# A graph attention layer on one core: query products in a bank of their own, their parts spread over two steps

## The chip, the cores and the metric

The kernel runs on one core of one Trainium2 chip. The metric is the device time of one execution in microseconds. Three runs of the kernel before gave a median of 1546.13 us (1540.45 to 1554.27).

## The reference

A graph has 3125 nodes with 128 features `x` and 100000 edges, sorted by their destination `dst`; each edge has a source `src` and one of five relations. Per relation there are query, key and value weights for eight heads of 16. The layer is an attention of every node over its incoming edges, separately for each relation, then a projection, a residual and two layer norms:

```
for r in range(5):
    q, k, v = x[dst] @ W_Q[r], x[src] @ W_K[r], x[src] @ W_V[r]
    logits  = (q * k).sum(-1) / 4 + attn_bias[r]          # masked to edges of relation r
    e       = exp(logits - segment_max(logits, dst))
    out    += segment_sum(e / (segment_sum(e, dst) + 1e-12) * v, dst)
h = out.reshape(3125, 128) @ out_proj_w.T + out_proj_b + x
y = layernorm(h) * ln_gamma + ln_beta
result = layernorm(x + y)
```

## The kernel before

All that counts is in `windowed_path`. It has a preamble, a main loop of 66 steps, and an end.

**Preamble.** Weights and `x` are loaded and turned on PE. `table(b)` makes, for each of 25 blocks of 128 nodes, a row of key and value for every node and relation, and SP stores it to the DRAM table `kv_d`. Small side jobs hang between the blocks by the dictionary `side`, among them `query_weights` (the turned query weights, L324 on PE and L328 on ACT) and `project_weights`. Behind the table the queries of the first four blocks are made: product on PE, then the three bf16 parts into which a float32 query is split (first: cast of the product; second: cast of the remainder; third: remainder minus second part), stored to `q_d`.

**Main loop.** Edges come in tiles of 128, four tiles to a group, three groups (twelve tiles) to a step; the last two steps have two groups. Several steps are under way at once; step `k` of the Python loop issues, for its own and its neighbours' groups:

- `products(k)` (DVE, L799), `logits(k)` (L832), `closed_lanes(k)` (L809): query times key, reduced to logits, lanes of other relations closed; `turn_logits` (PE, L860) and `keep_logits` (ACT, L875) turn them so that edges lie along the free axis; `scans(k)` (DVE, L881 and L884) and `less_max` (L891) give each segment's maximum and subtract it; `exps` (ACT, L899) and `turn_exps` (PE, L906) make the exponentials and turn them back.
- `weights(k-1)` (ACT, L916) and `weigh(k-1)` (DVE, L922) copy the exponentials and multiply the gathered values by them, into `wv`. `places` (ACT, L931 and L934) makes selection matrices, and `sums` (PE, L952 and L947) adds each group's rows up by segment, into the PSUM tile `both`.
- `norm(k-2)` (DVE, L964, L966, L968) divides by the totals, `relations(k-2)` (PE, L981) adds the five relations, `by_node(k-2)` (ACT, L985) copies the result to its nodes.
- `gather(k+3)` (POOL, L707): twelve indirect DMAs, one for each tile, that read rows of `kv_d`. The ring has a slot less than would be needed to be free of the current step: the last of the twelve writes to a slot that `weigh(k-1)` reads, and waits for it.
- `spot` (DVE, L764) and `spread_q` (PE, L778) spread the query rows over the edges of a tile. `take(k)` has SP load what they need, three steps ahead: the keys `kt` (L635), twelve pieces of query rows `qw` out of `q_d` (L642), the masks `mk` (L756). SP works through its queue in order.

The queries of blocks 4 to 24 are made inside the loop. `q_at` names the step at which `turn_q` and `turned` transpose the block (L717, L722). `half(k)` says that the next step handles its first three relations and the step after that the other two. In a step with a half, `remainder` and `second_part` stand between `logits` and `closed_lanes`, and `third_part` between `norm` and `relations`; the product and the first cast were issued at the end of the step before:

```
        if after[0] is not None:
            queries(*after)          # PE  L728, PSUM tile prq
            first_part(*after[:2])   # ACT L733
```

`remainder` is L737 (DVE), `second_part` L742 (ACT), `third_part` L746 (DVE). After the second half, `store_q` (SP, L608) writes the block's query rows to `q_d`. Blocks whose sums are complete are finished in the loop too: `project` (PE, L992), `residual`, `roots` (ACT, L1022), `norms`, `store_z` (SP, L1058). The order inside a step is written out by hand; each engine works through its instructions in that order, held by semaphores only.

PSUM has eight banks: three for the spread queries `qe`, two for `lt`, one for `ex`, one for `both`, and one, tagged `fin`, which transposes, query products, relation sums and projections take in turn.

**End.** After the loop the last two blocks' sums, norms and stores follow one another.

Of the kernel before, what the change touches and what calls it, by code (L numbers as in the profile page):

```python
# [17 lines left out]
P = 128  # L18
# [3 lines left out]
R = 5  # L22
# [112 lines left out]
def windowed_path(  # L135
# [111 lines left out]
    src_r = load_rows("src_r", src, 0)  # L247
    typ_r = load_rows("typ_r", edge_type, 0)
    load_x(10, 17)
    nc.sync.dma_start(wnq, w_q.rearrange("r k h d -> (r k) (h d)"))  # L250
# [151 lines left out]
    def table(b, xT):  # L402
        n_ = P if b < NT - 1 else 64
        kvs = work.tile([P, R * 2, H], F32, name="kvs", bufs=3)
        wf = wkv.rearrange("h r s c -> h (r s) c")
        for n, (c0, c1) in enumerate(((0, 4), (4, 8), (8, 10))):
# [8 lines left out]
        nc.sync.dma_start(  # L415
            kv_d[b * P * R : (b * P + n_) * R, :].rearrange("(p r) c -> p (r c)", r=R),
            kvs[:n_].rearrange("p s h -> p (s h)"),
        )

    kvrow = load.tile([HG, 2, GE], F32, name="kvrow")  # L420
    keyr = load.tile([HG, 2, GE], F32, name="keyr")
# [90 lines left out]
    def count_short():  # L512
        nc.vector.tensor_reduce(vio[:HG, 1:2], srt[:, :, : GE - SEG], AX.XY, ALU.add)
# [50 lines left out]
    def types(s, rs):  # L564
# [7 lines left out]
    side = {  # L572
        1: [begins],
        2: [weights_a],
        3: [lambda: query_weights(0)],
        4: [lambda: query_weights(8), weights_b],
        5: [lanes],
        6: [keys_a],
        7: [keys_c],
# [8 lines left out]
        16: [types(0, (0,)), project_weights],  # L588
        17: [types(0, (1,))],
        18: [types(0, (2,))],  # L590
        19: [types(0, (3,))],
# [88 lines left out]
    checks()  # L680
    pre.close()
# [31 lines left out]


    def turn_q(b):
        tp = ps.tile([P, P], F32, name="tp", tag="fin")
        nc.tensor.transpose(tp, xn[:, b, :], ident)  # L717
        live["tp", b] = tp

# [3 lines left out]

    def queries(b, c0, c1):
        if c0 == 0:
            live["q3", b] = flow.tile([P, R, 3, H], BF16, name="q3", bufs=1)
        pr = ps.tile([P, c1 - c0, H], F32, name="prq", tag="fin")
        nc.tensor.matmul(pr, live["xT", b], wq[:, c0:c1, :], start=True, stop=True)  # L728
        live["pr", b, c0] = pr, live["q3", b][:, c0:c1], c1 - c0
# [171 lines left out]
    def turn_exps(k):  # L901
        n = len(groups(k))
        ls = live.pop(("ls", k))
        ex = ps.tile([P, T * G3, HEADS], F32, name="ex")[:, : T * n]
        for t in range(T):
            nc.tensor.matmul(  # L906
                ex.rearrange("p (i t) k -> p t i k", t=T)[:, t],
                ls[: n * LANES, t * P : (t + 1) * P],
                gather_heads[: n * LANES, :n], start=True, stop=True,
            )  # L910
        live["ex", k] = ex
# [24 lines left out]

    def sums(g):
        k, i = AT[g]
        if i == 0 and ("both", k) not in live:
            live["both", k] = ps.tile([P, G3 * (PW + HEADS)], F32, name="both")  # L940
        pp = total(k)[:, i]
        at, wv = live.pop(("at", g)), live["wv", k]
        end = tiles_of(g) - 1
        for t in range(end + 1):
            if g and t == end:
                last, j = AT[g - 1]
                nc.tensor.matmul(  # L947
                    pp[:R], over[:, g, :],
                    live["wv", last][:, T * j + T - 1, :],
                    start=False, stop=False,  # L950
                )
            nc.tensor.matmul(  # L952
                pp[:WR], at[:, t, :], wv[:, T * i + t, :], start=(t == 0), stop=(t == end)
            )
        if i == 0:
            live.pop(("wv", k - 1), None)

    def total(k):
        return live["both", k][:, : G3 * PW].rearrange("p (g c) -> p g c", g=G3)

    def norm(k):
        n, pp = len(groups(k)), total(k)
        tot = live["both", k][:, G3 * PW :].rearrange("p (g c) -> p g c", g=G3)[:WR, :n]
        nc.vector.tensor_scalar_add(tot, pp[:WR, :n, H:PW], 1e-12)  # L964
        den = flow.tile([WR, G3, HEADS], F32, name="den", bufs=1)[:, :n]
        nc.vector.reciprocal(den, tot)  # L966
# [7 lines left out]
        live["o5", k] = o5  # L974
        live.pop(("both", k))

    def relations(k):
        o5 = live.pop(("o5", k))
        live["nodes", k] = nodes = ps.tile([P, G3, WN], F32, name="nodes", tag="fin")
        for i, g in enumerate(groups(k)):  # L980
            nc.tensor.matmul(nodes[:, i], o5[:, i], rsum[:WR], start=True, stop=True)  # L981

# [72 lines left out]

    def store_z(b):
        n = min(P, N - b * P)
        nc.sync.dma_start(out[b * P : b * P + n, :], live.pop(("z", b))[:n, :])  # L1058
# [5 lines left out]
    block_at = {k: b for b, k in done_at.items() if k < NST}  # L1064
    rest = [b for b in range(NT) if done_at[b] >= NST]


    q_from = {}
# [31 lines left out]

    for k in range(NST):
        new, old = k >= 1, k >= 2
        q0, (q, c0, c1), after = q_at.get(k), half(k), half(k + 1)
        done, rooted = block_at.get(k), block_at.get(k - 1)
        place_g, sum_g = list(groups(k - 1)), list(groups(k - 1))

# [46 lines left out]
        sum_next()  # L1153
# [19 lines left out]
    begun = rest[0] - 1  # L1173
    assert rest == [NT - 2, NT - 1] and done_at[begun] < k
    assert full_at(rest[0]) < G0[k] and len(groups(k)) == 2
    room = ps.tile([P, T * G3, H], F32, name="qe").rearrange("p n h -> p (n h)")
    live["both", k] = room[:, : G3 * (PW + HEADS)]
    places(G0[k])
    weights(k)
    places(G0[k] + 1)  # L1180
    norm(k - 1)
    relations(k - 1)
    by_node(k - 1)
    weigh(k)
    project(rest[0])
    for b in rest:
        shifted(b)
    roots(rest[0], 1, 2)
    norms(rest[0])
    store_z(begun)  # L1190
    sums(G0[k])
    residual(rest[0])
    roots(rest[0], 0, 1)
    sums(G0[k] + 1)
    norms(rest[0])
    norm(k)
    relations(k)
    by_node(k)
    project(rest[1])
    residual(rest[1])  # L1200
    roots(rest[1])
    norms(rest[1])
    store_z(rest[0])
    roots(NT, 1, 2)
    norms(NT)
    store_z(rest[1])

    ctx.close()

# [504 lines left out]
```

## Time and profile before

| what | value |
|---|---|
| median of three runs | 1546.13 us (1540.45 to 1554.27) |
| the profiled execution | 1546.65 us, its span 1544.9 us |
| preamble, to the first scan | 0 to 178.0 us |
| main loop, first to last scan | 178.0 to 1518.7 us |
| end | 1518.7 to 1544.9 us |
| busy: PE, DVE, POOL, ACT | 878.7, 883.9, 757.4, 620.8 us |
| mean granted TensorE clock | 0.667 |

PE, DVE, ACT, POOL and SP are the engines; PEld is PE's loading of weights. A row of a group names line, engine, operation, the tiles written and read, their shape and the count; then the busy time and the mean ns of one; then how long the engine had been idle just before such instructions and what ended that. A row of a timeline has the start, the duration, the engine, the line and the tiles, and in brackets the idle time before it and its releaser. "SPq" is SP's DMA queue. A row of windows gives a stretch, its length, and each engine's busy time. "remote" means that no event in the profile explains the release.

### The profile page before, as it was taken

How to read it: one execution, taken by the hardware profiler on the slowest of the kernel's cores; microseconds unless marked ns; L12 is line 12 of the kernel's file. 1: busy time of each engine (PE TensorE's matmuls, PEld its weight loads, DVE VectorE, ACT ScalarE, POOL GpSimd, SP SyncE). 2: the span in 40 equal slices, each digit the busy share in tenths (PEclk: the TensorE clock that was granted, in tenths of full speed). 3: DMA queues.
4: the chain of work that ended last, by engine and by line, in shares of the span. 5: the costliest groups of instructions: out<-in, count | busy, mean ns of one | idle time of the engine just before them, and what ended most of it. 6: DMA issues, size and time to landing. Idle time of an engine off the chain costs nothing. (4 is left out here: it accounts for less than half of the span.)

```text
span 1544.9 us, 17015 instructions
## 1 busy us (share of the span) xinstructions
PE 878.7 (57%) x4515; PEld 659.4 (43%) x4515; DVE 883.9 (57%) x1259; ACT 620.8 (40%) x1699; POOL 757.4 (49%) x850
## 2 busy tenths in 40 slices
PE   7920346545665555655556555565556655566686
PEld 4510234433444444443444434454444443344464
DVE  4831345645666545665556646565555655565686
ACT  3420233433453434443443434443433443444464
POOL 2067145445555555545555545555455545555510
PEclk9965566666666666666666666666666666666677
DMA  8663355434444445544454445544455434454420
GB/s 229 280 185 112 76 124 148 126 109 126 129 130 120 121 123 133 133 116 121 131 138 118 117 122 128 139 123 119 117 135 129 131 108 121 132 130 125 120 55 8
DMA packets 177099, 196.48 MB, mean 127 GB/s; under 512 B 122143, under 2 KB 137130, under 8 KB 176874
## 3 DMA queue, kind: packets, MB, share of 16 engines
q0 software_dynamic: 37728, 102.55, 25.4%
q1 hardware_dynamic: 138718, 91.65, 20.9%
q10 hardware_dynamic: 548, 1.11, 0.2%
q8 instruction: 38, 0.62, 0.2%
q14 instruction: 67, 0.55, 0.1%
HBM read 164.80 MB, written 30.40 MB: 126 GB/s over the span
## 5 line engine op out<-in xcount | busy, mean ns | idle before, releaser
L707 POOL DMA_INDIRECT kv_early<-kv_d,idx x474 | 453.2, 956 | 470.4 <-DVE wv L922 266.0
L952 PE MATMUL both<-wv,at 128*125 128x136 f32 x1552 | 393.5, 409 | 57.7 <-DVE wv L922 45.1
L707 POOL DMA_INDIRECT kv_late<-kv_d,idx x308 | 294.1, 955 | 250.1 <-DVE wv L922 163.3
L952 PEld LDWEIGHTS both<-wv,at 128*125 128x125 f32 x1552 | 316.7, 284 | 140.7 <-issue 75.3
L860 PE MATMUL lt<-ident,lx 128*120 128x128 f32 (+2 forms) x396 | 80.7, 361 | 374.9 <-DVE both L964 263.5
L931 ACT ACTIVATE at<-row_at,nkey 128x125 f32<-128x125 f32 x782 | 246.9, 388 | 0.0
L860 PEld LDWEIGHTS lt<-ident,lx 128*120 128x120 f32 (+2 forms) x396 | 51.5, 177 | 404.3 <-issue 357.9
L737 DVE TENSOR_TENSOR prq<-prq,q 128x384 f32<-128x384 f32 (+1 forms) x42 | 21.0, 500 | 349.6 <-ACT q L733 286.3
L733 ACT CAST q<-prq 128x384 bf16<-128x384 f32 (+1 forms) x42 | 17.9, 426 | 457.1 <-remote 416.4
L981 PE MATMUL nodes<-rsum,o 125*128 125x25 f32 x392 | 92.5, 380 | 119.1 <-DVE o L968 51.0
L981 PEld LDWEIGHTS nodes<-rsum,o 125*128 125x128 f32 x392 | 84.6, 312 | 132.0 <-DVE o L968 55.0
L934 ACT ACTIVATE at<-at 128x500 f32<-128x500 f32 x196 | 121.4, 619 | 6.2
L881 DVE TENSOR_TENSOR_SCAN lt<-mk,lt 120x640 f32<-120x640 bf16 (+1 forms) x66 | 98.3, 1489 | 36.2 <-DMA mk<-msk_d 35.7
L832 DVE TENSOR_REDUCE lt<-prod 128x96 f32<-128x1536 f32 (+1 forms) x66 | 115.0, 1742 | 2.2
L778 PE MATMUL qe<-qw,hot 120*128 120x128 bf16 x784 | 60.8, 221 | 74.6 <-DMA qw<-q_d 47.4
L947 PE MATMUL both<-wv,over 128*5 128x136 f32 x386 | 102.4, 360 | 0.0
L884 DVE TENSOR_TENSOR_SCAN lt<-mk,lt 120x640 f32<-120x640 bf16 (+1 forms) x66 | 98.7, 1495 | 2.2
L799 DVE TENSOR_TENSOR prod<-kv_early,qe 128x1536 f32<-128x1536 f32 (+3 forms) x53 | 71.3, 1346 | 41.6 <-DMA kv_late<-kv_d,idx 38.6
L916 ACT COPY wv<-ex 128x96 f32<-128x96 f32 (+1 forms) x66 | 15.1, 229 | 178.6 <-remote 165.2
L778 PEld LDWEIGHTS <-hot 120*128 120x128 bf16 x784 | 51.2, 105 | 77.3 <-issue 77.0
L922 DVE TENSOR_TENSOR wv<-kv_early,ex 128x1536 f32<-128x1536 f32 (+1 forms) x40 | 69.3, 1733 | 25.2 <-ACT wv L916 25.2
L875 ACT COPY ls<-lt 120x512 f32<-120x512 f32 (+1 forms) x66 | 39.0, 591 | 103.0 <-PE lt L860 99.1
(169 smaller groups left out, 1087.2 us busy)
## 6 DMA issues: line engine op xcount, KB each, us to landing
qw<-q_d SPq DMA_DIRECT2D x784, 30.0 KB
kt<-key_d SPq DMA_DIRECT2D x63, 360.0 KB
kv_d<-kvs SPq DMA_DIRECT2D x24, 640.0 KB
q_d<-q SPq DMA_DIRECT2D x25, 480.0 KB
mk<-msk_d SPq DMA_DIRECT2D x64, 150.2 KB
kv_early<-kv_d,idx POOLq DMA_INDIRECT x474
kv_late<-kv_d,idx POOLq DMA_INDIRECT x308
out<-z SPq DMA_DIRECT2D x24, 64.0 KB
```

The costliest lines, as they stand in the source:

```text
L707: nc.gpsimd.indirect_dma_start(out=kv[:, at, :], out_offset=None, in_=kv_d[:, :], in_offset=bass.IndirectOffsetOnAxis(ap=idx[:, q % T, q / ...
L778: nc.tensor.matmul(dest[j], hot[:, j * P : (j + 1) * P], qw[:, j, :], start=True, stop=True)
L799: nc.vector.tensor_tensor(prod[:, n:m], kv[:, c0:c1, :H], qe[:, n:m], op=ALU.mult)
L832: nc.vector.tensor_reduce(lg, heads(live.pop(("prod", k))[:, :m]), AX.X, ALU.add)
L860: nc.tensor.transpose(live["lt", k][: n * LANES, c : c + w], live["lx", k][p : p + w, j : j + n].rearrange("p g r k -> p (g r k)"), ident[ ...
L881: nc.vector.tensor_tensor_scan(lt, mk[:n, :WIDE], lt, -BIG, op0=ALU.add, op1=ALU.max)
L884: nc.vector.tensor_tensor_scan(lt[:, ::-1], mk[:n, WIDE:0:-1], lt[:, ::-1], -BIG, op0=ALU.add, op1=ALU.max)
L931: nc.scalar.activation(at[:, t, :], row_at[:, :WR], AF.Abs, bias=nkey[:, t, g : g + 1], scale=1.0)
L934: nc.scalar.activation(at[:, :n], at[:, :n], AF.Relu, bias=1.0, scale=-1.0)
L947: nc.tensor.matmul(pp[:R], over[:, g, :], live["wv", last][:, T * j + T - 1, :], start=False, stop=False,)
L952: nc.tensor.matmul(pp[:WR], at[:, t, :], wv[:, T * i + t, :], start=(t == 0), stop=(t == end))
L981: nc.tensor.matmul(nodes[:, i], o5[:, i], rsum[:WR], start=True, stop=True)
```

## The change

Four things are changed, and all of the loop's order that depends on them.

1. PSUM: `ex`, the projection `pj` and the transpose `tp` share one bank, `mid`; the relation sums `nodes` lie in spare columns of `both`'s bank for the following step; the query product `prq` alone is left in `fin`. The tile of query parts, `q3`, has two buffers.
2. The query work: in the step of a half, the product and the first cast come after the projection, ahead of the second group's sums and of `less_max` and `exps`; `remainder` at the end of that step. `second_part` is at the start of the next step, `third_part` between `by_node` and `weigh` of that next step, and there `store_q`.
3. The preamble: the three weight arrays are loaded in two pieces each, K on ACT's queue, V and Q on SP's; the table's last block is stored in three pieces; `query_weights` comes after the table, `project_weights` after the first queries.
4. The end: the block `begun` is projected and added up in the loop but finished after it; the last group's `weigh` and `sums` come ahead of `norm(k-1)`; a block's last rows that are no multiple of 16 are stored on ACT's queue.

The core of the diff:

```diff
-    for s, a in enumerate((w_k, w_v)):
-        nc.scalar.dma_start(
-            wn[s * R * HEADS : (s + 1) * R * HEADS, :], a.rearrange("r k h d -> (r k) (h d)")
-        )
-    load_x(0, 4)
+    def load_weights(queue, t, a):
+        rows = a.rearrange("r k h d -> (r k) (h d)")
+        for p0, p1 in ((0, 32), (32, R * HEADS)):
+            queue.dma_start(t[p0:p1, :], rows[p0:p1])
+
+    load_weights(nc.scalar, wn[: R * HEADS, :], w_k)
+    load_x(0, 2)
+    load_weights(nc.sync, wn[R * HEADS :, :], w_v)
+    load_x(2, 4)
...
+            done = (c0, c1) if b == NT - 1 else (0, c1)
+            if b == NT - 1 or c1 == 2 * R:
+                nc.sync.dma_start(
+                    rows[:, done[0] * H : done[1] * H],
+                    kvs[:n_, done[0] : done[1]].rearrange("p s h -> p (s h)"),
+                )
...
     turned_q(1)
+    query_weights(0)
+    query_weights(8)
     for n, (b, c0, c1) in enumerate(halves):
...
+    project_weights()
     count_short()
...
+    mid = ps.tile([P, 4 * P], F32, name="mid")
...
-        tp = ps.tile([P, P], F32, name="tp", tag="fin")
+        tp = mid[:, 3 * P :]
...
-            live["q3", b] = flow.tile([P, R, 3, H], BF16, name="q3", bufs=1)
+            live["q3", b] = flow.tile([P, R, 3, H], BF16, name="q3", bufs=2)
...
-        ex = ps.tile([P, T * G3, HEADS], F32, name="ex")[:, : T * n]
+        ex = mid[:, : T * n * HEADS].rearrange("p (t k) -> p t k", k=HEADS)
...
+    def both(k):
+        if ("both", k) not in live:
+            live["both", k] = ps.tile([P, G3 * (PW + HEADS + WN)], F32, name="both")
+        return live["both", k]
...
-    def relations(k):
+    def relations(k, room=None):
         o5 = live.pop(("o5", k))
-        live["nodes", k] = nodes = ps.tile([P, G3, WN], F32, name="nodes", tag="fin")
+        if room is None:
+            room = both(k + 1)[:, G3 * (PW + HEADS) :]
+        live["nodes", k] = nodes = room[:, : G3 * WN].rearrange("p (g w) -> p g w", g=G3)
...
-    def project(b, tag="fin"):
+    def project(b):
         n = min(P, N - b * P)
-        pj = ps.tile([P, H], F32, name="pj", tag=tag)
+        pj = mid[:, (1 + b % 2) * P :][:, :H]
...
     for k in range(NST):
         new, old = k >= 1, k >= 2
-        q0, (q, c0, c1), after = q_at.get(k), half(k), half(k + 1)
+        q0, (q, c0, c1), (q1, d0, _) = q_at.get(k), half(k), half(k - 1)
...
+        if q1 is not None:
+            second_part(q1, d0)
         place_next()
         if new:
             weights(k - 1)
...
         logits(k)
-        if q is not None:
-            remainder(q, c0)
-            second_part(q, c0)
         closed_lanes(k)
...
         if old:
             norm(k - 2)
-        if q is not None:
-            third_part(q, c0)
-        if old:
             relations(k - 2)
             by_node(k - 2)
+        if q1 is not None:
+            third_part(q1, d0)
+            if d0:
+                store_q(q1)
         if new:
             weigh(k - 1)
...
         scans(k)
+        if k == done_at[begun]:
+            project(begun)
         if done is not None:
             project(done)
+        if q is not None:
+            queries(q, c0, c1)
+            first_part(q, c0)
+        sum_next()
         less_max(k)
         exps(k)
...
+        if k < NST - 1:
+            sum_next()
+        turn_exps(k)
         sum_next()
-        if after[0] is not None:
-            queries(*after)
-            first_part(*after[:2])
-        turn_exps(k)
+        if q is not None:
+            remainder(q, c0)
...
         take(k)
-        if c0:
-            store_q(q)
...
+    weigh(k)
+    sums(G0[k])
     norm(k - 1)
-    relations(k - 1)
+    sums(G0[k] + 1)
+    relations(k - 1, room[:, GE:])
     by_node(k - 1)
-    weigh(k)
-    project(rest[0])
...
```

More of the change, by code (lines that the diff above doesn't have):

```diff
@@ L249, in windowed_path @@
     load_x(10, 17)
-    nc.sync.dma_start(wnq, w_q.rearrange("r k h d -> (r k) (h d)"))
+    load_weights(nc.sync, wnq, w_q)
     load_x(17, NT - 1)
@@ L405, in table @@
         wf = wkv.rearrange("h r s c -> h (r s) c")
+        rows = kv_d[b * P * R : (b * P + n_) * R, :].rearrange("(p r) c -> p (r c)", r=R)
         for n, (c0, c1) in enumerate(((0, 4), (4, 8), (8, 10))):
@@ L414, in table @@
                 nc.vector.tensor_copy(kvs[:, c0:c1, :], pr[:, : c1 - c0, :])
[L415 to L418, printed above, removed]
+            done = (c0, c1) if b == NT - 1 else (0, c1)
[4 more added lines that the diff above has]
+                )
     kvrow = load.tile([HG, 2, GE], F32, name="kvrow")
@@ L574, in windowed_path @@
         2: [weights_a],
-        3: [lambda: query_weights(0)],
-        4: [lambda: query_weights(8), weights_b],
+        4: [weights_b],
         5: [lanes],
@@ L587, in windowed_path @@
         15: [spills, late_ends],
-        16: [types(0, (0,)), project_weights],
+        16: [types(0, (0,))],
         17: [types(0, (1,))],
@@ L938, in sums @@
         k, i = AT[g]
-        if i == 0 and ("both", k) not in live:
-            live["both", k] = ps.tile([P, G3 * (PW + HEADS)], F32, name="both")
         pp = total(k)[:, i]
@@ L956, in sums @@
             live.pop(("wv", k - 1), None)
+    def both(k):
+        if ("both", k) not in live:
+            live["both", k] = ps.tile([P, G3 * (PW + HEADS + WN)], F32, name="both")
+        return live["both", k]
     def total(k):
-        return live["both", k][:, : G3 * PW].rearrange("p (g c) -> p g c", g=G3)
+        return both(k)[:, : G3 * PW].rearrange("p (g c) -> p g c", g=G3)
     def norm(k):
         n, pp = len(groups(k)), total(k)
-        tot = live["both", k][:, G3 * PW :].rearrange("p (g c) -> p g c", g=G3)[:WR, :n]
+        tot = live["both", k][:, G3 * PW : G3 * (PW + HEADS)].rearrange("p (g c) -> p g c", g=G3)[:WR, :n]
         nc.vector.tensor_scalar_add(tot, pp[:WR, :n, H:PW], 1e-12)
@@ L1057, in store_z @@
         n = min(P, N - b * P)
-        nc.sync.dma_start(out[b * P : b * P + n, :], live.pop(("z", b))[:n, :])
+        z = live.pop(("z", b))
+        m = n // 16 * 16
+        nc.sync.dma_start(out[b * P : b * P + m, :], z[:m, :])
+        if m < n:
+            nc.scalar.dma_start(out[b * P + m : b * P + n, :], z[m:n, :])
     done_at = {b: AT[full_at(b)][0] + 2 for b in range(NT)}
@@ L1063, in windowed_path @@
         done_at[b] = max(done_at[b], done_at[b - 1] + 1)
-    block_at = {k: b for b, k in done_at.items() if k < NST}
-    rest = [b for b in range(NT) if done_at[b] >= NST]
+    begun = max(b for b in range(NT) if done_at[b] < NST)
+    block_at = {k: b for b, k in done_at.items() if b < begun}
     q_from = {}
@@ L1152, in windowed_path @@
             residual(done)
-        sum_next()
+        if k == NST - 1:
+            for b in range(begun, NT):
+                shifted(b)
+            residual(begun)
         if q0 is not None:
@@ L1172, in windowed_path @@
     k = NST - 1
-    begun = rest[0] - 1
-    assert rest == [NT - 2, NT - 1] and done_at[begun] < k
-    assert full_at(rest[0]) < G0[k] and len(groups(k)) == 2
+    rest = [begun, begun + 1, begun + 2]
+    assert rest[-1] == NT - 1 and done_at[begun - 1] < k - 1 and done_at[begun] < k
+    assert full_at(rest[1]) < G0[k] and len(groups(k)) == 2
     room = ps.tile([P, T * G3, H], F32, name="qe").rearrange("p n h -> p (n h)")
-    live["both", k] = room[:, : G3 * (PW + HEADS)]
+    live["both", k] = room[:, : G3 * (PW + HEADS + WN)]
     places(G0[k])
     weights(k)
+    roots(begun)
     places(G0[k] + 1)
+    weigh(k)
+    sums(G0[k])
     norm(k - 1)
-    relations(k - 1)
+    sums(G0[k] + 1)
+    relations(k - 1, room[:, GE:])
     by_node(k - 1)
-    weigh(k)
-    project(rest[0])
[L1186 to L1195, printed above, removed]
+    project(rest[1])
+    norms(begun)
+    store_z(begun - 1)
     norm(k)
-    relations(k)
+    relations(k, room[:, 2 * GE :])
     by_node(k)
-    project(rest[1])
     residual(rest[1])
@@ L1202, in windowed_path @@
     norms(rest[1])
-    store_z(rest[0])
+    store_z(begun)
+    project(rest[2])
+    residual(rest[2])
+    roots(rest[2])
+    norms(rest[2])
+    store_z(rest[1])
     roots(NT, 1, 2)
     norms(NT)
-    store_z(rest[1])
+    store_z(rest[2])
     ctx.close()
```

## The prediction

> **What bounds the kernel now.** I read the page first: its busy times, its groups, and what ended their idle time.
>
> ```profile
> span 1544.9 us, 17015 instructions
> PE 878.7 (57%) x4515; PEld 659.4 (43%) x4515; DVE 883.9 (57%) x1259; ACT 620.8 (40%) x1699; POOL 757.4 (49%) x850
> L707 POOL DMA_INDIRECT kv_early<-kv_d,idx x474 | 453.2, 956 | 470.4 <-DVE wv L922 266.0
> L737 DVE TENSOR_TENSOR prq<-prq,q 128x384 f32<-128x384 f32 (+1 forms) x42 | 21.0, 500 | 349.6 <-ACT q L733 286.3
> L733 ACT CAST q<-prq 128x384 bf16<-128x384 f32 (+1 forms) x42 | 17.9, 426 | 457.1 <-remote 416.4
> ```
>
> No engine is full, so a chain of waits repeats once per step. The third row closes it: POOL's gathers wait for `weigh` (L922), because the last of a step's twelve overwrites the slot that `weigh` reads. The last two rows are the query work that the change moves: 286.3 us of DVE's waits hang on a cast that waits for something the profile calls remote. Next, the busy time by stretches: the 21 steps that handle three relations of a query block (A), the 21 that handle two (B), the 14 between with neither (dots), each row the sum over its steps from scan to scan (L881), and a stretch near the end.
>
> ```profile
> sum 454.28, PE 250.15 PEld 192.80 DVE 266.67 ACT 187.06 POOL 240.35; mean PE 11.91 PEld 9.18 DVE 12.70 ACT 8.91 POOL 11.45
> sum 479.82, PE 276.47 PEld 214.17 DVE 260.82 ACT 188.65 POOL 240.84; mean PE 13.17 PEld 10.20 DVE 12.42 ACT 8.98 POOL 11.47
> sum 274.29, PE 159.13 PEld 124.87 DVE 173.16 ACT 128.42 POOL 160.53; mean PE 11.37 PEld 8.92 DVE 12.37 ACT 9.17 POOL 11.47
> 1457.85:1472.40 14.55, 13.13 (x66) 10.10 (x66) 12.04 (x17) 9.37 (x27) 7.67 (x8) 0.62 0.51 124
> ```
>
> So A takes 454.28/21 = 21.63 us, B 22.85, a dot 19.59, though busy times are alike. A step with 8 gathers instead of 12 takes 14.55: gathers matter. The timeline shows how; first a dot:
>
> ```profile
> 861.26 0.95 POOL L707 DMA_INDIRECT kv_early<-kv_d,idx  x1 [8.77 <-DVE wv L922]
> 868.37 0.97 PE L906 MATMUL ex<-gather_heads,ls 120*128 120x24 f32 x8
> 869.71 9.91 SPq L642 DMA_DIRECT2D qw<-q_d  x8
> 875.13 0.94 POOL L707 DMA_INDIRECT kv_early<-kv_d,idx  x1 [0.30 <-issue]
> 878.30 0.24 ACT L916 COPY wv<-ex 128x96 f32<-128x96 f32 x1 [9.26 <-remote]
> 878.58 1.75 DVE L922 TENSOR_TENSOR wv<-kv_early,ex 128x1536 f32<-128x1536 f32 x1 [4.82 <-ACT wv L916]
> ```
>
> PE finishes the exponentials (L906) at 869.34, yet ACT, which needs nothing else, reads them at 878.30: 2.23 us after the last gather's end (876.07), 17.04 after POOL's restart (861.26). While gathers and SP's row loads (L642) run together, PE's results reach nobody. Then A, from the release on:
>
> ```profile
> 829.05 0.95 POOL L707 DMA_INDIRECT kv_late<-kv_d,idx  x1 [0.30 <-issue]
> 832.35 0.48 ACT L733 CAST q<-prq 128x384 bf16<-128x384 f32 x1 [11.05 <-remote]
> 832.86 0.57 DVE L737 TENSOR_TENSOR prq<-prq,q 128x384 f32<-128x384 f32 x1 [8.70 <-ACT q L733]
> 833.34 0.65 DVE L809 TENSOR_TENSOR lx<-lt,shut 128x480 f32<-128x480 f32 x1
> 835.18 0.56 DVE L746 TENSOR_TENSOR q<-prq,q 128x384 bf16<-128x384 f32 x1 [0.17 <-ACT q L742]
> 835.66 1.74 DVE L922 TENSOR_TENSOR wv<-kv_early,ex 128x1536 f32<-128x1536 f32 x1
> ```
>
> Release again 2.35 us after the gathers' end, and only then the chain cast, remainder, closed lanes, norm, third part, weigh: 5.05 us from 832.35 to 837.40, against 2.03 in the dot. B is worse, because ACT's root (L1022) and a placement (L931, up to L916) stand behind the stuck cast:
>
> ```profile
> 854.68 0.37 ACT L733 CAST q<-prq 128x256 bf16<-128x256 f32 x1 [12.46 <-remote]
> 855.08 1.28 ACT L1022 ACT_TABLE_LOAD   x1
> 858.38 0.22 ACT L916 COPY wv<-ex 128x96 f32<-128x96 f32 x1
> 859.25 1.74 DVE L922 TENSOR_TENSOR wv<-kv_early,ex 128x1536 f32<-128x1536 f32 x1
> 859.79 0.38 SPq L608 DMA_DIRECT2D q_d<-q  x1
> ```
>
> From 854.68 to 860.99 are 6.31 us. The bound is thus gathers (fixed), their drain (fixed), and what stands behind the release.
>
> **The change, part by part.**
>
> *Query work spread over two steps.* The product now has a bank of its own and is multiplied right after a block's projection, behind the first group's sums; ACT's first cast stands before the exponentials, DVE's remainder at the step's end, ACT's second cast at the start of the next step, the third part between that step's norm and weigh. What speaks for the cast being in time is how PE's other early results travel before the row loads begin:
>
> ```profile
> 820.01 0.27 PE L717 MATMUL tp<-ident,xn 128*128 128x128 f32 x1
> 821.05 0.25 ACT L722 COPY xTq<-tp 128x128 f32<-128x128 f32 x1
> 821.57 0.81 PE L728 MATMUL prq<-wq,xTq 128*128 128x384 f32 x2
> 823.73 13.13 SPq L642 DMA_DIRECT2D qw<-q_d  x12
> ```
>
> The transpose reaches ACT within 0.8 us; the product, finished at 822.4 and followed by the loads at 823.73, is stuck until 832.35. Moved behind the first group's sums, it ends some 3 us after weigh (in the dot above at about 864: weigh ends 860.99, the sums start 861.14 in the row under *The banks*), over 5 us ahead of the loads (869.71). The casts and the remainder (0.48, 0.57) then lie under the 9 us in which ACT and DVE wait for the release anyway; without that cover they would cost 0.48 + 0.57 + 0.48 again, 1.5 us per step. Only the third part stays near the path. A dot whose norm is late shows the path without it:
>
> ```profile
> 812.12 0.19 DVE L964 TENSOR_SCALAR both<-both 125x24 f32<-125x24 f32 x1 [7.07 <-remote]
> 813.17 1.75 DVE L922 TENSOR_TENSOR wv<-kv_late,ex 128x1536 f32<-128x1536 f32 x1
> ```
>
> Release to weigh's end is 2.80 there (812.12 to 814.92). With the third part (0.56, or 0.43 by its shape in B) and POOL's 0.27 the cycle is 17.04 + 2.8 + 0.5 + 0.27 = 20.6; where the norm comes early, as in the dot at 878.58, the third part is hidden too and the cycle is 17.04 + 2.03 + 0.27 = 19.34. I take 20.6 for all 42 steps, the end that counts its cost, and leave dots alone: (454.28 + 479.82) - 42 x 20.6 = 934.1 - 865.2 = **-68.9 us**; at 19.34 it would be -121.9.
>
> *The store of the finished queries* (SP, `q_d`) now waits for the third part of the step after B, but stands in SP's queue ahead of that step's key load and twelve row loads (L642). In 21 steps these are held until just before weigh. Row loads feed a step two later, so nothing starves at once. Two ends: without loads beside the gathers there is no jam and the step falls to POOL's twelve issues, 12 x 1.26 = 15.1 us (861.26 to 875.13 is eleven such intervals); or the loads, held back, run at the start of the following step and jam it early. I take 0, since the two partly cancel; the ends are rivals 2 and 3.
>
> *The banks.* Exponentials, projection and transpose share one bank, the relation sums lie in spare columns of the totals' bank. PE already has such a wait here:
>
> ```profile
> 860.90 0.61 ACT L985 COPY oT<-nodes 128x25 f32 x3 [1.54 <-PE nodes L981]
> 861.14 1.70 PE L952 MATMUL both<-wv,at 128*125 128x136 f32 x6 [0.28 <-ACT oT L985]
> ```
>
> Should the sums wait for the whole copy, they would start at 861.51 instead of 861.14, 0.37 us later, and L906 behind them at 868.7 instead of 868.4, nine us ahead of the release: 0. It would cost 64 x 0.37 = 24 us with that cover gone. The Trainium skill, in "PSUM — Partial Sum Buffer", section "PSUM bank collisions raise a hardware error", asks for PSUM to be guarded by bank, not by address, since engines touching other columns of a bank collide too. It speaks against packing banks; the row agrees that PE waits for ACT there, in this case by 0.28 us.
>
> *The start.* The sixteen weight turns leave the table loop, where PE sets the pace, and run behind it, under the gathers.
>
> ```profile
> 83.68 1.04 POOL L707 DMA_INDIRECT kv_early<-kv_d,idx  x1 [71.40 <-DVE q L664]
> L324 PE MATMUL wpq<-ident,wnq 40*128 40x40 f32 x16 | 2.1, 281 | 0.0
> ```
>
> The first gather comes 2.1 us sooner: **-2.1**. Weights in pieces: 0 taken; bounds -1.5 (PE's idle ahead of the first weight turns) and +1 for more issues on SP.
>
> *The end.* Sums of the last group come straight after weigh.
>
> ```profile
> 1525.06 1.22 DVE L922 TENSOR_TENSOR wv<-kv_early,ex 128x1024 f32<-128x1024 f32 x1 [0.55 <-ACT wv L916]
> 1528.19 1.72 PE L952 MATMUL qe<-wv,at 128*125 128x136 f32 x6
> ```
>
> They can start 1.9 us earlier (1526.28); a third block to finish gives some back: **-1.5**, bounds -3 and +1.5.
>
> Sum on the profiled execution's own 1546.65: 1546.65 - 68.9 - 2.1 - 1.5 = **1474.2**. That execution lies 0.5 us above the median of the runs shown (1546.13; 1540.45 to 1554.27), so I leave it.
>
> **Rivals.**
>
> 1. The gain is hidden anyway: the release follows the chain, not the gathers. For it: both ends move together from step to step. Against: release is 2.23, 2.35 us after the last gather, whatever the step holds. Only start and end would count: 1543.
>
> 2. Held loads free the step. For it: the 14.55 us step, and PE's promptness before the loads. 21 x (20.6 - 15.1) = 116 less: 1358; with only half of them free, 1416.
>
> 3. Slower: loads held behind the third part run from the start of the next step, and the product's arrival is jammed there. That step always has a first cast (next block's A or B). Stuck, it holds remainder, products (1.75), the reduction (1.76), closed lanes, norm and weigh behind the release: 0.48 + 0.57 + 1.75 + 1.76 + 0.65 + 1.05 + 1.74 + 0.27 = 8.3, so 25.3 instead of 20.6. In 21 steps: +99, or 1573; in all 42 steps 1672. It turns the gain of 72.5 (68.9 + 2.1 + 1.5) into a loss from 16 stuck steps on (72.5/4.7). For it: SP needs 13 to 15 us per step already, so held loads spill over. Against: the same hold would free the step before (then 1573 - 116 = 1457). The two middle rows of that price are DVE's, from the dot:
>
> ```profile
> 866.69 1.75 DVE L799 TENSOR_TENSOR prod<-kv_late,qe 128x1536 f32<-128x1536 f32 x1
> 868.48 1.76 DVE L832 TENSOR_REDUCE lt<-prod 128x96 f32<-128x1536 f32 x1
> ```
>
> 4. The shared banks' 24 us are not covered, because steps become shorter: 1498.
>
> **How the numbers follow.** Forecast 0.45, with its own range 1421 (early norms) to 1498; rival 1 0.09, rival 2 0.16, rival 3 0.25, rival 4 0.05. This kernel's measurement can tell about 1% from no change. Faster: 0.45 + 0.16 + 0.05 = 0.66; within 1%: 0.09; slower: 0.25. The range goes from 1400 (half of rival 2 and more lies below) to 1575, with rival 3 in 21 steps inside and the heavier stalls outside.
>
> **What would show it.** Right: the first cast no longer waits for "remote", the wait of the first DVE subtraction for it falls from 286 us to under 30, A and B steps last 19.3 to 20.6 us, and the release still follows the gathers by 2.2 us. Wrong: steps behind a query store that last 25 us with the first cast stuck (rival 3), steps of 15 us (rival 2), or A and B still above 21.5 with the cast prompt (rival 1).

## The result, and the profile after

The changed kernel took 1479.49 us (median of 4 runs, 1479.0 to 1481.54) against 1546.67 us: a ratio of 0.9566, 95% interval 0.9522 to 0.961. The profiled execution took 1479.0 us. That is 4.3% less; 1474.2 had been forecast.

The page of the changed kernel, its span and the groups that now carry the waits (lines are about ten higher than before: L926 is `weights`, L932 `weigh`, L977 the first instruction of `norm`):

```profile
span 1477.2 us, 17102 instructions
L717 POOL DMA_INDIRECT kv_early<-kv_d,idx x474 | 453.6, 957 | 433.3 <-DVE wv L932 228.5
L977 DVE TENSOR_SCALAR both<-both 125x24 f32<-125x24 f32 (+1 forms) x65 | 12.4, 191 | 392.0 <-remote 305.5
L926 ACT COPY wv<-mid 128x96 f32<-128x96 f32 (+1 forms) x66 | 15.7, 238 | 470.2 <-remote 385.2
```

The groups kept apart by shape, for the cast (L743, was L733) and the remainder (L747, was L737) of the larger half:

```profile
L747 DVE TENSOR_TENSOR prq<-prq,q 128x384 f32<-128x384 f32 x21 | 11.9, 567 | 20.4 <-ACT q L743 12.0 <-issue 8.4
L743 ACT CAST q<-prq 128x384 bf16<-128x384 f32 x21 | 10.1, 479 | 32.0 <-PE prq L738 24.4 <-issue 7.6
```

"Remote" is gone from the cast, in the smaller half too, and in both halves together DVE's first subtraction waits 13.4 us for the cast (12.0 and 1.4) instead of 286.3. The hold-up itself, that PE's results are taken up only behind the last gather, has not gone: it has moved to `weights` and `norm`, which had it before almost only in steps without query work (17 of the 20 waits of `weights`, all 10 of `norm`). Busy time in the same three kinds of steps as in the prediction (A, B, dots; sums over 21, 21, 14), from scan to scan:

```profile
sum 422.38, PE 241.69 PEld 189.77 DVE 253.07 ACT 178.74 POOL 241.02; mean PE 11.51 PEld 9.04 DVE 12.05 ACT 8.51 POOL 11.48
sum 430.00, PE 282.60 PEld 208.51 DVE 267.32 ACT 201.35 POOL 240.80; mean PE 13.46 PEld 9.93 DVE 12.73 ACT 9.59 POOL 11.47
sum 287.99, PE 175.56 PEld 133.81 DVE 182.45 ACT 130.48 POOL 161.36; mean PE 12.54 PEld 9.56 DVE 13.03 ACT 9.32 POOL 11.53
```

A lasts 20.11 us (21.63 before), B 20.48 (22.85), a dot 20.57 (19.59): together 1140.4 us against 1208.4, 68.0 less. The names are those of the prediction, but the change moves each half's query work one such stretch on: the first half's now lies in B, the second half's in the stretch behind it, which is a dot (14 times) or an A (7 times). Sorted by that, first the 14 stretches without query work, then the 42 with it:

```profile
sum 277.74, PE 153.50 PEld 120.71 DVE 162.00 ACT 113.34 POOL 160.16; mean PE 10.96 PEld 8.62 DVE 11.57 ACT 8.10 POOL 11.44
sum 862.63, PE 546.35 PEld 411.38 DVE 540.84 ACT 397.22 POOL 483.02; mean PE 13.01 PEld 9.79 DVE 12.88 ACT 9.46 POOL 11.50
```

That is 19.84 us without and 20.54 us with query work. The timeline of one dot, in which a smaller half goes from its product to its third part:

```profile
658.76 0.94 POOL L717 DMA_INDIRECT kv_late<-kv_d,idx  x1 [5.82 <-DVE wv L932]
661.46 1.06 PE L738 MATMUL prq<-wq,xTq 128*128 128x256 f32 x2
662.56 0.37 ACT L743 CAST q<-prq 128x256 bf16<-128x256 f32 x1 [0.18 <-PE prq L738]
662.96 0.43 DVE L747 TENSOR_TENSOR prq<-prq,q 128x256 f32<-128x256 f32 x1 [0.22 <-issue]
663.18 16.45 SPq L648 DMA_DIRECT2D qw<-q_d  x12
664.78 0.35 ACT L752 CAST q<-prq 128x256 bf16<-128x256 f32 x1
665.81 0.97 PE L916 MATMUL mid<-gather_heads,ls 120*128 120x24 f32 x8
672.74 0.95 POOL L717 DMA_INDIRECT kv_late<-kv_d,idx  x1 [0.30 <-issue]
676.01 0.19 DVE L977 TENSOR_SCALAR both<-both 125x24 f32<-125x24 f32 x1 [6.93 <-remote]
676.10 0.24 ACT L926 COPY wv<-mid 128x96 f32<-128x96 f32 x1 [9.15 <-remote]
677.05 0.41 DVE L756 TENSOR_TENSOR q<-prq,q 128x256 bf16<-128x256 f32 x1
677.38 1.75 DVE L932 TENSOR_TENSOR wv<-kv_late,mid 128x1536 f32<-128x1536 f32 x1
```

The product reaches ACT at once; casts and remainder are done before the hold-up. The exponentials, finished by PE at 666.78, reach ACT at 676.10: 2.41 us after the last gather's end (673.69). From `norm`'s start to `weigh`'s end are 3.12 us, of which the third part takes 0.41.

Where the time went, by the first scan, the scans after it and the end: first scan 181.47 instead of 178.02 (+3.45); 56 steps -68.0; the last eight steps -3.5; end 26.6 instead of 26.1 (+0.5). That adds up to the 67.7 us by which the spans differ.

### The profile page after: what moved, and what is told of

It reads as the page before. It is cut to its first block, busy times and chain, and to the rows that moved or that the text cites. A ratio compares the mean times of both kernels' runs of the same rounds, so it can differ in the third digit from the quotient of the medians.

```text
span 1477.2 us, 17102 instructions
## 1 busy us (share of the span) xinstructions
PE 884.8 (60%) x4515; PEld 655.1 (44%) x4515; DVE 885.4 (60%) x1258; ACT 624.3 (42%) x1696; POOL 758.4 (51%) x850
## 5 line engine op out<-in xcount | busy, mean ns | idle before, releaser
L960 PE MATMUL both<-wv,at 128*125 128x136 f32 x1552 | 376.7, 392 | 71.1 <-ACT oT L1000 43.8
L960 PEld LDWEIGHTS both<-wv,at 128*125 128x125 f32 x1552 | 307.6, 271 | 162.9 <-issue 78.1
L977 DVE TENSOR_SCALAR both<-both 125x24 f32<-125x24 f32 (+1 forms) x65 | 12.4, 191 | 392.0 <-remote 305.5
L926 ACT COPY wv<-mid 128x96 f32<-128x96 f32 (+1 forms) x66 | 15.7, 238 | 470.2 <-remote 385.2
L996 PE MATMUL both<-rsum,o 125*128 125x25 f32 x384 | 89.6, 378 | 179.1 <-DVE o L981 126.5
L996 PEld LDWEIGHTS both<-rsum,o 125*128 125x128 f32 x384 | 83.7, 315 | 199.7 <-remote 126.0
L788 PE MATMUL qe<-qw,hot 120*128 120x128 bf16 x784 | 68.5, 228 | 113.0 <-issue 59.5
L955 PE MATMUL both<-wv,over 128*5 128x136 f32 x386 | 98.6, 348 | 0.0
L916 PE MATMUL mid<-gather_heads,ls 120*128 120x24 f32 (+1 forms) x528 | 69.4, 270 | 40.4 <-issue 26.9
L916 PEld LDWEIGHTS mid<-gather_heads,ls 120*128 120x128 f32 (+1 forms) x528 | 68.5, 202 | 43.0 <-issue 28.9
```

Source lines behind the costliest of these rows:

```text
L788: nc.tensor.matmul(dest[j], hot[:, j * P : (j + 1) * P], qw[:, j, :], start=True, stop=True)
L916: nc.tensor.matmul(ex.rearrange("p (i t) k -> p t i k", t=T)[:, t], ls[: n * LANES, t * P : (t + 1) * P], gather_heads[: n * LANES, :n], s ...
L955: nc.tensor.matmul(pp[:R], over[:, g, :], live["wv", last][:, T * j + T - 1, :], start=False, stop=False,)
L960: nc.tensor.matmul(pp[:WR], at[:, t, :], wv[:, T * i + t, :], start=(t == 0), stop=(t == end))
```

## The experiments

The runs fell on different chips, and that turned out to matter more than any edit. On the chip of runs e5 to e8 the kernel before took 1549.15 us, as on that of the result; on the chips of e1 to e4 and of e9 to e12 the same kernel took 1115.18 and 1112.91. Each ratio below is against runs on its own chip; I call the first kind the chips with the hold-up, the second those without.

**e1 and e6: banks alone.** Everything of the change except the place of the query parts.

```diff
-        if q is not None:
-            queries(q, c0, c1)
-            first_part(q, c0)
...
+        if after[0] is not None:
+            queries(*after)
+            first_part(*after[:2])
         turn_exps(k)
...
+        if q is not None:
+            remainder(q, c0)
+            second_part(q, c0)
         closed_lanes(k)
```

> The changed kernel with its banks, its start and its end, but with the query parts where the kernel before had them: product and first cast at the end of the step before, remainder and second part between logits and closed lanes, third part behind the norm. Theory (the gain is the chain of query work that stood behind the release): A and B steps are back at 21.6 and 22.9 us, the whole back at about 1547 us (1479.5 + 68). Rival (the gain is the banks: transposes, relation sums and projections no longer take turns in one bank): most of the gain stays, 1480 to 1500 us. If both count, the time lies between and says how much each gives.

> As the first run of this kernel: banks, start and end of the change, query parts where they were. On a chip with the hold-up: theory (moved query parts are the gain) about 1547 us, rival (banks) 1480 to 1500. On a chip without it: 0.997 of the kernel before, as in the first run, about 1112 us.

Without the hold-up (e1): 1112.34 us, ratio 0.9972 (0.9959 to 0.9984). With it (e6): 1545.29 us, ratio 0.9982 (0.9953 to 1.0011). The groups of e6, then the same group of e1:

```profile
L747 DVE TENSOR_TENSOR prq<-prq,q 128x384 f32<-128x384 f32 (+1 forms) x42 | 21.0, 500 | 331.4 <-ACT q L743 274.9 <-issue 56.5
L743 ACT CAST q<-prq 128x384 bf16<-128x384 f32 (+1 forms) x42 | 17.9, 425 | 445.8 <-remote 413.3 <-DMA qw<-q_d 13.6 <-PE qe L788 10.3
```

```profile
L743 ACT CAST q<-prq 128x384 bf16<-128x384 f32 (+1 forms) x42 | 17.9, 426 | 136.1 <-PE prq L738 130.1 <-PE both L960 6.0
```

With the query parts back in their places, the wait for "remote" is back (413.3 us; 416.4 before the change), and so are A and B steps of 21.8 and 22.6 us. The gain is the move of the query parts; the banks, the start and the end together give 0.2%, within the interval. By the code the banks are a condition of the move, since with one bank for transposes and products a product could not be kept over a step; no run here tries that. Without the hold-up the same order of the same instructions shows no remote wait at all.

**e5: the changed kernel once more.**

> The changed kernel itself, because the chip of the last four runs took 1115 us for the kernel before where the first chip took 1546: there SP issued 25 row loads in 18 us beside the gathers, on the first chip in 73 us. Theory: the change's gain is made of waits for results held up beside the gathers; where row loads take 0.7 us as on that second chip and a step is POOL's twelve issues (15.1 us), the gain is within 1%: 1100 to 1120 us; where they take over 1 us as on the first chip, about 1480 against 1546. Rival (the gain is the shorter chain itself, on any chip): 4% on both, about 1070 us on a chip like the second.

It fell on a chip with the hold-up: 1477.81 us, ratio 0.9532 (0.9487 to 0.9576). The result repeats. The changed kernel itself was not run on a chip without the hold-up, so what it gives there was not measured. Four variants of it that were (e4, e10, e11 and e12 below) took 1119 to 1122 us there, against 1113 to 1115 for the kernel before, so the rival's 1070 is unlikely.

**e3 and e7: one row load instead of twelve.** What holds up PE's results?

```diff
-            for j, f in enumerate(starts(first15, a, b, SPE)):
-                nc.sync.dma_start(qw[:, a + j - B0[k], :], q_d[bass.ds(f, 3 * QR), :])
+        (f,) = starts(first15, B0[k], B0[k] + 1, SPE)
+        rows = q_d[bass.ds(f, 3 * QR), :]
+        nc.sync.dma_start(qw[:, :n, :], rows[:, None, :].to_broadcast([3 * QR, n, H]))
```

> The changed kernel with one DMA in place of a step's twelve row loads: it moves as many bytes in as many pieces, but always the first tile's rows, so the logits of the other tiles are those of wrong queries; the time of every engine's work is the same. Theory (PE's results are held up while SP issues its loads beside the gathers): with one issue instead of twelve there is no jam, a step falls to POOL's twelve issues, about 15.1 to 16 us, and the 56 steps lose 250 to 290 us: about 1190 to 1230 us. Rival (the release is set by the gathers alone, 2.2 us behind the last): steps stay at 20.4 us, 1475 to 1480 us. Second rival (it is the bytes of the loads, not their issues): also 1475 to 1480, with the one load's landing as late as the last of twelve.

> The changed kernel with one DMA instead of a step's twelve row loads, as many bytes, always the first tile's rows (so the queries of the other tiles are wrong ones). On a chip with the hold-up: theory (it needs SP's many issues beside the gathers) steps of 15 to 16 us, 1110 to 1230 us in all; rival (gathers alone hold up PE's results) 1475 to 1480. On a chip without it: 1115 us, as in the first run.

Without the hold-up 1114.99 us, one run, against 1115.18 of the kernel before. With it 1416.07 us, one run: far above the 1110 to 1230 of my theory, and some 60 us below the rival's 1475 to 1480. So neither time came out, and the trace has to tell which mechanism did. The timeline of e7, around one release, and its start, where POOL issues the first 60 gathers on end; the last row is the DMA queue of the gathers (packets, MB, share of the DMA engines' time), the only one with transfers between 132 and 160 us:

```profile
656.69 0.95 POOL L717 DMA_INDIRECT kv_late<-kv_d,idx  x1 [0.30 <-issue]
660.04 0.24 ACT L926 COPY wv<-mid 128x96 f32<-128x96 f32 x1 [9.80 <-remote]
```

```profile
121.09 1.38 PE L870 MATMUL lt<-ident,lx 128*120 128x128 f32 x6 [1.53 <-issue]
129.20 0.70 SPq L766 DMA_DIRECT2D mk<-msk_d  x1
159.34 0.95 POOL L717 DMA_INDIRECT kv_late<-kv_d,idx  x1 [0.30 <-issue]
165.77 0.59 ACT L885 COPY ls<-lt 120x512 f32<-120x512 f32 x1 [70.12 <-remote]
170.75 0.36 SPq L641 DMA_DIRECT2D kt<-key_d  x1
q0 software_dynamic: 1074, 2.95, 37.0%
```

Release still comes 2.40 us after the gathers' end (657.64), though SP has only three loads a step. In the start PE has turned the logits by 122.47, and SP issues nothing from 129.90 to 170.75. Still ACT reads them only at 165.77, 43.3 us after PE's end and 5.5 us behind the last gather (160.29). So on this chip the gathers alone keep results held up; whether they alone also begin it is not shown, since SP was still loading at 122. The twelve loads cost something beside that: without them the first scan came at 166.4 instead of e5's 181.4 us, and the 56 steps took 1095.5 instead of e5's 1143.2, as `norm` came more than 0.5 us ahead of `weights` in 49 of 60 steps instead of 8.

**e8: the start as before.** Weights in one piece, four blocks of x first, query weights inside the table loop.

```diff
-    load_weights(nc.scalar, wn[: R * HEADS, :], w_k)
-    load_x(0, 2)
-    load_weights(nc.sync, wn[R * HEADS :, :], w_v)
-    load_x(2, 4)
+    for s, a in enumerate((w_k, w_v)):
+        nc.scalar.dma_start(
+            wn[s * R * HEADS : (s + 1) * R * HEADS, :], a.rearrange("r k h d -> (r k) (h d)")
+        )
+    load_x(0, 4)
...
+        3: [lambda: query_weights(0)],
+        4: [lambda: query_weights(8), weights_b],
```

> The changed kernel with the start of the kernel before: weights in one piece each and all of K and V on ACT's queue, four blocks of x loaded first, query weights turned inside the table loop, project weights beside block 16. In the changed kernel the table began 1.7 us later (14.6 against 12.9 us), saved 2.1 us in the loop, and its row loads began 4.7 us later (103.1 against 98.4). Theory (query products later means row loads later, and these set the first scan where they are slow): first scan 3 to 4 us sooner on a chip with the hold-up, 1476 us; 1 us or less on a chip without it. Rival (the moved weight turns help, as the prediction had it): 2 us longer.

1477.24 us, ratio 0.9531 (0.9485 to 0.9577), against 1477.81 of e5 on the same chip: no difference that can be told. The profiled run shows the mechanism, though. SP's row loads and the first scan, of e8:

```profile
99.38 73.15 SPq L650 DMA_DIRECT2D qw<-q_d  x25
179.03 1.50 DVE L890 TENSOR_TENSOR_SCAN lt<-mk,lt 120x640 f32<-120x640 bf16 x1 [24.66 <-DMA mk<-msk_d]
```

The same two rows of the changed kernel:

```profile
103.07 72.06 SPq L648 DMA_DIRECT2D qw<-q_d  x25
181.47 1.50 DVE L891 TENSOR_TENSOR_SCAN lt<-mk,lt 120x640 f32<-120x640 bf16 x1 [21.56 <-DMA mk<-msk_d]
```

The first scan follows the row loads: 2.4 us sooner with the old start, where 3 to 4 had been expected. That the whole did not follow by as much stays within the spread of the runs.

**e2 and e9: the product late.** Only product and first cast moved back, ahead of `turn_exps` in their own step.

```diff
         sum_next()
         less_max(k)
...
+        if q is not None:
+            queries(q, c0, c1)
+            first_part(q, c0)
         turn_exps(k)
```

> The changed kernel with one thing moved: the product and its first cast stand at the end of their step, just ahead of the turned exponentials, no longer ahead of the second group's sums; remainder, second and third part stay where the change puts them. Theory (the product's arrival ahead of the row loads is what counts): the first cast is stuck until the release again, and now holds remainder, products, reduction, closed lanes, norm and weigh behind it: 25.3 us in all 42 steps, 1479.5 + 42 x 4.7 = about 1677 us. Rival (only the place of the later parts counts, the arrival does not): 1480 to 1490 us.

> As the earlier run of this kernel: product and first cast at the end of their step, the rest of the change as it is. On a chip with the hold-up (where the kernel before takes about 1546 us): theory (the product has to reach ACT before the hold-up begins) the first cast is stuck and holds DVE's chain behind it: 25.3 us in the 42 steps, about 1677 us. Rival (only the places of the later parts count): 1478 to 1490. On a chip without it: 1152, as in the first run.

Both fell on chips without the hold-up: 1152.45 and 1152.67 us, one run each, against 1115.18 and 1112.91. The timeline of e2:

```profile
491.37 0.81 PE L738 MATMUL prq<-wq,xTq 128*128 128x384 f32 x2
492.21 0.48 ACT L743 CAST q<-prq 128x384 bf16<-128x384 f32 x1 [5.45 <-PE prq L738]
492.73 0.57 DVE L747 TENSOR_TENSOR prq<-prq,q 128x384 f32<-128x384 f32 x1 [5.17 <-ACT q L743]
```

DVE reaches the remainder 5.17 us before its cast, and everything of the next step queues behind it. So the early place of the product is needed for an ordinary reason too: the remainder at the step's end has to find its input. What this order costs under the hold-up (1677 expected) was not run there.

**e4, e10, e11: weigh first.** `weigh` ahead of `norm`, `relations` and the third part; in e11 also product and first cast ahead of `norm`.

```diff
+        if new:
+            weigh(k - 1)
         if old:
             norm(k - 2)
...
-        if new:
-            weigh(k - 1)
```

> The changed kernel with weigh ahead of norm, relations and the third part on DVE, PE and ACT. Theory (only what stands between the release and weigh's end sets the step): norm (1.05) and third part (0.5) leave that path, every step falls to 19.34 us from a mean of 20.4: 56 x 1.0 = 56 us less, about 1423 us. Rival (the sums and the product, which now come 2.5 us later on PE, run into the row loads, and the first cast is stuck): 25 us in part of the 42 steps, 1500 us and more.

> As the earlier run of this kernel: weigh ahead of norm, relations and third part. On a chip with the hold-up: theory (a step is the release plus what stands ahead of weigh's end) 19.3 us in every step against 20.4: 56 us less, about 1422 us. Rival (product 2.5 us later on PE runs into the hold-up) 25 us in part of the steps, 1500 and more. On a chip without it: 1.005 of the kernel before, as in the first run.

> Weigh first, then third part, product and first cast, and only then norm, relations and copy to the nodes. The product comes about 1 us after weigh's end, ahead of the relation sums. On a chip with the hold-up: theory 19.3 us in every step and no stuck cast, about 1422 us, also where the kernel with weigh first alone fails; rival (PE's later sums run into the hold-up instead, and the exponentials with them) 1480 and more. On a chip without the hold-up: 1110 to 1125 us.

All three fell on chips without the hold-up: 1121.73 us, ratio 1.0052 (1.0036 to 1.0069); 1119.84 us, 1.0058 (1.004 to 1.0075); 1120.92 us, 1.006 (1.0044 to 1.0077). There is nothing to win there by an earlier `weigh`, since POOL is not waiting for it (its gathers' waits for `weigh` come to 0.6 us in all in e1); the 56 us expected under the hold-up stay open.

**e12: the gathers in two.**

```diff
+            if k >= KVA and q == B0[k] + 5:
+                nc.gpsimd.tensor_copy(seen, live["lx", k - KVA][0:1, 1, 0, 0:1])
```

> The changed kernel with POOL's gathers in two halves: the sixth after each restart waits, by a copy of one element, until DVE has closed the lanes of the step (about 10.6 us after weigh's end). Theory (results are held up only by a long run of gathers on end, the one-load run having shown that the row loads matter little): the first half drains, the exponentials are read at once, weigh ends about 13 us after the last, and a step is POOL's 15.1 us plus a pause of about 2: 17 to 18 us, about 1310 to 1350 us in all. Rival (results come through only when a whole group of twelve has gone): POOL ends 2 us later, steps of 22 us, about 1570 us. On a chip without the hold-up: 2 us a step more, about 1220 us.

Without the hold-up: 1119.43 us, ratio 1.0048 (1.002 to 1.0077), not the 1220 expected there. POOL's timeline:

```profile
469.84 0.94 POOL L721 DMA_INDIRECT kv_early<-kv_d,idx  x1 [0.30 <-issue]
470.78 0.18 POOL L719 COPY seen<-lx 1x1 f32<-1x1 f32 x1
471.12 0.97 POOL L721 DMA_INDIRECT kv_early<-kv_d,idx  x1 [0.16 <-issue]
```

The copy finds its lanes closed already and costs 0.03 us (471.12 - 469.84 is 1.28 instead of 1.25): here DVE runs ahead of POOL. It is not free of other effects: ACT's copy into the same tile (L868) now waits for POOL's, 172.0 us in all. Its question, whether shorter runs of gathers let results through, was not put to a chip with the hold-up.

## Why the prediction was right, and where it was not

**The loop, right in mechanism and size.** Forecast were 42 steps of 20.6 and 14 of 19.59, 1139.5 us; measured 42 of 20.54 and 14 of 19.84, 1140.4. Where the hold-up sets the release it still follows the gathers by about 2.4 us, and what stands behind it is what the cycle adds. e6 shows the cause: with the parts put back, A and B are back. I had the third parts in A and B; they lie in B and in the stretch after, often a dot. So the dots rose by 1 us and A fell further than the working said; the sum is the same, 42 such steps. That I took 20.6 and not 19.34 was a choice between two ends: it holds because `norm` mostly came late (more than 0.5 us ahead of `weights` in 12 of 60 steps), which the prediction had not shown.

**What causes the hold-up, wrong.** The prediction named gathers and row loads together. e7 shows that the gathers alone are enough to keep results held up. It did not hurt the sum, which used only the measured 17.04 us; it did make rival 2 look possible.

**The store of the queries, wrong.** I had read that it would hold a step's row loads behind the third part. SP's queue in the step shown above:

```profile
679.68 0.73 SPq L766 DMA_DIRECT2D mk<-msk_d  x1
681.47 0.04 SPq L614 DMA_DIRECT2D q_d<-q  x1
681.56 0.45 SPq L641 DMA_DIRECT2D kt<-key_d  x1
```

The row loads of that step (663.18 to 679.63) stand ahead of the store, and SP reaches it 4 us after the third part's end (677.46). I was off by one step. Nothing is held; the cost of 0 was right for another reason than "they cancel", and rivals 2 and 3 rested on a wait that is not there. No step was near 15 or 25 us.

**Banks, right.** e6 gives 0.9982 with the interval across 1. The rule of the Trainium skill to guard PSUM by bank and not by address ("PSUM — Partial Sum Buffer", "PSUM bank collisions raise a hardware error") brought no cost that shows in the time here: PE's sums wait 43.8 us in all for ACT's copy of the relation sums (L1000) instead of 11.6. The wait of 0.28 us in the prediction is no case of that rule, since there the two tiles lay in different banks.

**The start, wrong in sign.** -2.1 forecast, +3.45 measured. The first gather did not come sooner (84.08 against 83.68), and the table began later. The first row is of the kernel before, the second of the changed one:

```profile
12.94 4.58 PE L408 MATMUL pr<-wkv,xT 128*128 128x512 f32 x6
```

```profile
14.61 4.29 PE L413 MATMUL pr<-wkv,xT 128*128 128x512 f32 x6 [0.36 <-DVE xT L305]
```

That is 1.7 us later, outside the bounds of -1.5 and +1 that I had set for the weights; two blocks of x now stand behind them, but which of the edits to the start does it was not separated. On the chip of e5 to e8 the table began at 14.00 to 14.46 with the new start (e5, e6, e7) and at 13.68 with the old (e8). Nor did moving the weight turns out of the loop show its 2.1 us: from the table's start to the first gather are 70.7 us before and 69.5 after, but 69.5 with the old start in e8 and 69.3 to 70.6 with the new one in e5 to e7. That the turns set the loop's pace is not borne out. And the gathers' start was the wrong thing to cost: the first scan waits for masks behind 25 row loads, which began 4.7 us later since the query products did; e8 shows that part.

**The end, too hopeful.** -1.5 forecast, +0.5 measured. Of the changed kernel:

```profile
1456.95 1.22 DVE L932 TENSOR_TENSOR wv<-kv_early,mid 128x1024 f32<-128x1024 f32 x1 [1.24 <-ACT wv L926]
1458.23 1.17 PE L960 MATMUL qe<-wv,at 128*125 128x136 f32 x6 [1.88 <-DVE wv L932]
1460.53 11.59 SPq L1075 DMA_DIRECT2D out<-z  x4
1470.09 0.34 DVE L1065 TENSOR_SCALAR z<-y,mv,sd 53x128 f32<-53x128 f32 x1
```

And before:

```profile
1528.91 10.71 SPq L1058 DMA_DIRECT2D out<-z  x3
1539.01 0.34 DVE L1050 TENSOR_SCALAR z<-y,mv,sd 53x128 f32<-53x128 f32 x1
```

The sums do start 1.28 us after `weigh`'s start instead of 3.13, the forecast 1.9 us. Of that, 0.8 is left at the last z (19.54 us after the last scan instead of 20.35); the rest probably goes to the third block. Then SP's last store, now 48 rows with 5 more on ACT, is issued until 1472.12, 1.69 us after z's end, where the 53 rows in one took 0.27. I had costed the split store at nothing. The split is not the whole of it: SP's issue of the same 48 rows took 1.66 us here, 1.31 in e5 and 1.47 in e8, but 0.33 in e6 and 0.34 in e7. What makes it long stays open.

In the last eight steps I had forecast nothing; they gave 3.5 us, and that was luck. The loop, the start and the end came out 0.9, 5.6 and 2.0 us above the forecast, and these 3.5 us brought the whole back to 4.8 above it.

## What to carry to other kernels

Look for what stands behind a late release, not for what is busy: 42 casts of 0.4 us cost 68 us because each stood where results came late and a chain stood behind it; moved to where its input is there at once, the same query work costs a step 0.7 us (20.54 against 19.84) instead of 2.6. For a term of the start or the end, find the wait that ends last before costing anything ahead of it. And ask whether the wait is the kernel's or the chip's: time the unchanged kernel on more than one.

## What the runs showed of the hardware

The same kernel before took 1546 to 1549 us on the chips of the result and of e5 to e8, and 1113 to 1115 on two others. POOL's gathers take the same on both (957 ns, and 956 in e1). What differs is what runs beside them: 25 row loads take 73 us (98.36 to 171.44) on the one and, in SP's queue of e1,

```profile
99.85 18.36 SPq L648 DMA_DIRECT2D qw<-q_d  x25
```

18 us on the other; and PE's results, which reach ACT or DVE without a "remote" wait on the second, come about 2.4 us after the last gather on the first. There, too, a result that comes early in a run of gathers gets through: the product of the changed kernel, 3.8 us after POOL's restart, reaches ACT at once (662.56). Why some chips do this, the runs don't show. It is left open whether it belongs to the chip or to a state that it was in during these runs.
